# The scores' scaling and the experts' numbers of the slots with one operand in PSUM

## The chip, the cores and the metric

The kernel runs on one core of a Trainium2 chip. Its time is the device time of one launch in microseconds. A core has five engines with a queue of instructions each, worked off in order: TensorE (PE, matrix products and transposes), VectorE (DVE), ScalarE (ACT), GpSimd (POOL) and SyncE (SP, which here only issues DMA transfers). An instruction waits at the head of its queue until those whose results it needs have signalled.

## The reference

The input is `x` of 4 images, 384 channels, 32 x 32 positions, in fp32. Two layers follow, each a mixer and a feed-forward part with residual sums:

```python
x = x + selective_scan_block(ln_c(x))        # 4 scan directions, 16 states, softplus, norm, gelu
t = to_tokens(x)
scores = ln_t(t) @ gate_w + gate_b           # 4 experts
probs = softmax(scores)
masked = probs of the two best, normalised
t = t + sum_e masked[e] * (gelu(ln_t(t) @ w1[e] + b1[e]) @ w2[e] + b2[e])
x = x + attention(ln_c(from_tokens(t)))      # 8 heads of 64
t = to_tokens(x)
t = t + gelu(ln_t(t) @ kron(c_fc_1, c_fc_2).T) @ kron(c_proj_1, c_proj_2).T
```

The change lies in the routing: the scores, and the list that says which expert's weights each slot of tokens takes.

## The kernel before

**The stages.** The scan is done for the four images (batches) in turn. A batch has 4 directions in 2 halves of 512 positions, so there are 32 units; a unit has 3 chunks of 128 channels and 4 groups of states, so there are 384 groups in all. A group works so: ACT makes the decays `da` in PSUM (L443), POOL multiplies `bx` (L434, twice a group), DVE runs the recurrences (L448, four times, and small copies of the carries, L454 and L459), POOL and DVE multiply by the output coefficients (L462 once, L455 twice), and PE adds up the states (L469, eight matmuls in the profile). Between the units lie the projections (L332, L359, L389 to L398). The coefficients come back from DRAM, spread over the partitions, by DMA on SP (`bcs` L344, `dtr` L418).

**The tail of a batch** runs beside the scan of the next ones:
- `route`, called for batch 0 by itself and for batch b + 1 inside the tail of batch b: `spread` (from L620) transposes the tokens (L641), takes raw scores from the same bank (L643), statistics (L654, L655), and 1/sqrt of the variance by ACT as `rstd` (L151, L152). Then it scales the scores (L658), adds the bias (L659), makes `less`, the negative product of mean and rstd (`less_mean`, L546 and L547), and calls `places`. POOL then scatters the normalised tokens to rows sorted by expert with 16 indirect transfers (L675), each about 1.27 us after the one before.
- `places` (L682 to L847) does some sixty small DVE operations on tiles of at most 128 columns: ranks of the experts, counts, the position of each token (`pos`, L818), its weight (L846), and at the end the expert of each slot (`expert`, L844). Its scratch `area` is one PSUM bank of tag `o`, which `small` cuts up; what isn't in `area` is in SBUF.
- `experts`: 11 slots a batch, each with a fetch of 8 weight blocks of 576 KB on SP, whose address is loaded from `expert` (L858), a gather of token rows (`xs`, L891), transposes (L900), two products (L921 and L937), and a store.
- `combine` gathers the two rows of each token on POOL (L967), weighs and adds them on PE (L975) and DVE (L979). `prologue` normalises (stats, `less_mean`, L992) and transposes (L999). Then come `attention` (projection L1024, scores L1047, exponentials L1052, sums L1096) and `last_layers` (L1144, z L1163, hidden layer L1184, f_acc L1197, output L1207 and L1211).

**What sets the order.** The program is written once and a scheduler with a model of the engines' times then places each instruction in its engine's queue. So the order of all queues depends on what the model makes of every operation, and instructions far from an edit move with it. Routing, combining and the last layers have high priority. Tiles are shared by tags: `p`, `o` and `s` are PSUM banks, and with one buffer of tag `p` while the scan runs, `less_ps`, `cnt_ps`, `fo_ps` and others take turns; `o` holds `places`, `y_ps`, `o_acc` or `f_acc`.

In the text a "group" is one of the 384 scan groups, numbered by the L469 matmuls of PE's queue. Line numbers are those of the kernel before.

Of the kernel before, what the change touches and what calls it, by code (L numbers as in the profile page):

```python
# [12 lines left out]
ALU = mybir.AluOpType  # L13
AX = mybir.AxisListType
# [3 lines left out]
P = 128  # L18
# [14 lines left out]
NE = 4  # L33
# [8 lines left out]
NFULL = TOP * L // SLOT  # L42
NHALF = (NROW - NFULL * SLOT) // P
# [6 lines left out]
MB = L // P  # L50
# [65 lines left out]
class Body:  # L116
# [425 lines left out]
    def less_mean(self, mean, rstd, room, tag):  # L542

        less = room.tile([P, MB], tag, "less")
        ps = room.bank("p", "less_ps")[:, :MB]
        self.nc.scalar.copy(ps, rstd)  # L546
        self.nc.vector.scalar_tensor_tensor(less, mean, -1.0, ps, op0=ALU.mult, op1=ALU.mult)  # L547
        return less

# [68 lines left out]
    def spread(self, b, x1, room):  # L620


        nc = self.nc
        src = x1[b].rearrange("(c p) l -> p c l", p=P)
        st = room.tile([P, MB, 6], "r_st", "st")
        mv = room.tile([P, MB, 2], "r_mv", "mv")
        rstd = room.tile([P, MB], "r_rstd", "rstd")
        sc = room.tile([P, MB, NE], "sc", "sc")


        for m in [*range(MB // 2, MB, 2), *range(0, MB // 2, 2)]:
            x = room.tile([P, DC, 2 * P], "k4", "x")
            nc.sync.dma_start(out=x, in_=src[:, :, m * P : (m + 2) * P])
            xt = room.tile([P, 2, D], "k4", "xt")

            both = room.two("tt_ps") if b == 0 else None
            for o in range(2):
                ps = room.bank("p", "tt_ps") if both is None else both[:, o, :]
                cols = slice(o * P, (o + 1) * P)
                for c in range(DC):  # L640
                    nc.tensor.transpose(ps[:, c * P : (c + 1) * P], x[:, c, cols], self.ident)  # L641
                for c in range(DC):
                    nc.tensor.matmul(  # L643
                        ps[:, D : D + NE], x[:, c, cols], self.wg[:, c, :],
                        start=(c == 0), stop=(c == DC - 1),
                    )
                if both is None:
                    nc.scalar.copy(xt[:, o, :], ps[:, :D])
                    nc.vector.tensor_copy(sc[:, m + o, :], ps[:, D : D + NE])
            if both is not None:  # L650
                nc.scalar.copy(xt, both[:, :, :D])
                nc.vector.tensor_copy(sc[:, m : m + 2, :], both[:, :, D : D + NE])
            for o in range(2):
                nc.vector.bn_stats(st[:, m + o, :], xt[:, o, :])  # L654
                nc.vector.bn_aggr(mv[:, m + o, :], st[:, m + o, :])  # L655
            nc.sync.dma_start(out=self.tokens(b)[:, m : m + 2, :], in_=xt)
        self.inverse_root(rstd, mv[:, :, 1], self.eps5)
        nc.vector.tensor_mul(sc, sc, rstd.unsqueeze(2).to_broadcast([P, MB, NE]))  # L658
        nc.vector.tensor_add(sc, sc, self.bg.unsqueeze(1).to_broadcast([P, MB, NE]))  # L659
        less = self.less_mean(mv[:, :, 0], rstd, room, "r_less")  # L660
        pos, gate, expert = self.places(sc, room)

        placed = []
        for m in range(MB):
            if m % 2 == 0:
                xt = room.tile([P, 2, D], "k4", "xt")
                nc.sync.dma_start(out=xt, in_=self.tokens(b)[:, m : m + 2, :])
            nc.scalar.activation(  # L670
                xt[:, m % 2, :], xt[:, m % 2, :], AF.Identity,
                bias=less[:, m : m + 1], scale=rstd[:, m : m + 1],
            )
            for k in range(TOP):
                put = nc.gpsimd.indirect_dma_start(  # L675
                    out=self.rows[b][:, :],
                    out_offset=bass.IndirectOffsetOnAxis(ap=pos[:, k, m : m + 1], axis=0),
                    in_=xt[:, m % 2, :], in_offset=None,
                ).ins
                for other in placed:  # L680
                    self.tc.declare_no_dep(put, other, reason="rows of different tokens")
                for other in self.zeroed:  # L682
                    self.depend(put, other)
                placed.append(put)
        return (pos, gate), (expert, placed)

    def places(self, sc, room):


        nc = self.nc  # L690
# [51 lines left out]
        ps = room.bank("p", "cnt_ps")  # L742
# [27 lines left out]
        first = room.tile([P, 2, NE + 1], "g_first", "g_first")  # L770
        nc.vector.memset(first[:, :, :1], 0.0)
        for e in range(NE):
            nc.vector.tensor_add(first[:, :, e + 1], first[:, :, e], used[:, :, e])
        pairs, odd = first[:, 0], first[:, 1]
        more = room.tile([P, 1], "g_more", "g_more")
# [14 lines left out]
            op0=ALU.mult, op1=ALU.add,  # L790
# [13 lines left out]
            op0=ALU.mult, op1=ALU.add,  # L804
# [14 lines left out]

        def later(n, before, name):
            flags = room.tile([P, n, NE - 1], "g_" + name, "g_" + name)
            nc.vector.tensor_tensor(
                flags, self.slot_at[:, :n].unsqueeze(2).to_broadcast([P, n, NE - 1]),
                before[:, 1:NE].unsqueeze(1).to_broadcast([P, n, NE - 1]), op=ALU.is_ge,
            )
            return flags

        ef = room.tile([P, NSLOT], "g_ef", "g_ef")  # L830
        nc.vector.tensor_reduce(
            ef[:, : NFULL + 1], later(NFULL + 1, pairs, "later"), AX.X, ALU.add
        )
        half = room.tile([P, 2, NHALF], "g_half", "g_half")
        nc.vector.tensor_reduce(half[:, 0], later(NHALF, odd, "lone"), AX.X, ALU.add)
        nc.vector.tensor_sub(
            half[:, 1, :2], ef[:, NFULL : NFULL + 1].to_broadcast([P, 2]), half[:, 0, :2]
        )
        nc.vector.tensor_sub(half[:, 1, 2:], half[:, 0, : NHALF - 2], half[:, 0, 2:])
        nc.vector.scalar_tensor_tensor(  # L840
            ef[:, NFULL:], half[:, 1], more, half[:, 0], op0=ALU.mult, op1=ALU.add
        )
        expert = room.sb.tile([P, NSLOT], I32, tag="g_expert", name="g_expert", bufs=2)
        nc.vector.tensor_copy(expert, ef)  # L844
# [140 lines left out]
    def prologue(self, xt, xn, room):  # L985


        nc = self.nc
        mean, rstd = self.stats(xt, self.eps6, room)
        less = self.less_mean(mean, rstd, room, "less")  # L990
        for m in range(MB):
            nc.scalar.activation(  # L992
                xn[m], xt[:, m, :], AF.Identity, bias=less[:, m : m + 1], scale=rstd[:, m : m + 1]
            )
        xc = room.tile([P, DC, L], "k12", "xc")
        for c in range(DC):
            ps = room.two("tc_ps")
            for m in range(MB):
                nc.tensor.transpose(  # L999
                    ps[:, m // 4, m % 4 * P : (m % 4 + 1) * P], xn[m][:, c * P : (c + 1) * P],  # L1000
                    self.ident,
                )
            nc.scalar.copy(xc[:, c, :], ps.rearrange("p o l -> p (o l)"))
        return xc
# [443 lines left out]
```

## Time and profile before

| | |
|---|---|
| three runs | 4393.62, 4397.94, 4407.22 us; median 4397.94 |
| the profiled execution | 4396.59 us; span in the profile 4394.8 us |
| granted TensorE clock, mean | 0.852 |
| busy | PE 78%, POOL 69%, DVE 66%, ACT 56%, weight loads 37% |
| last scan step of DVE (L455) ends | 3517 us |
| first expert transposes (L900) of batches 0, 1 and 3 | 910, 1940 and 3615 us |
| traffic | 684.81 MB by DMA, mean 156 GB/s |

How to read it: the page gives busy time by engine, the span in 40 slices with the busy share in tenths, the chain of work that ended last, and the costliest groups of instructions with their mean length and the idle time before them. A row of a timeline has the start in us, the length, engine, line, operation, output and inputs, shape and count, and in brackets how long the engine stood idle before it and what ended that. In group rows the last columns are busy us, mean ns of one, and idle us before. An instruction's length runs from its start to its end as the profiler records them, so a wait for something other than a semaphore is part of the length.

### The profile page before, as it was taken

The numbers are of one execution on the slowest core, as the hardware profiler recorded it, in microseconds if no ns is written. First come the engines' busy times: TensorE is split into PE (matmuls) and PEld (weight loads), VectorE is DVE, ScalarE is ACT, GpSimd is POOL, SyncE is SP. The second block draws the span as 40 slices with busy tenths as digits, with TensorE's granted clock in tenths as the row PEclk, the third lists the DMA queues.
The fourth block names the chain that finished last, engine by engine and source line by source line (L and its number), as shares of the span: only waits on it lengthen the run. The fifth ranks groups of instructions, "written<-read, shape, count | busy, mean of one in ns | idle before, by whom it ended". The sixth has DMA issues, their size and how long they took to land.

```text
span 4394.8 us, 47123 instructions
## 1 busy us (share of the span) xinstructions
PE 3448.4 (78%) x13980; PEld 1647.6 (37%) x13980; DVE 2901.9 (66%) x4256; ACT 2479.0 (56%) x4402; POOL 3050.7 (69%) x1475
## 2 busy tenths in 40 slices
PE   6545545479996897679997888758998789999997
PEld 2111113145553232235554322314555435556433
DVE  5889996878866868968887677978787720002102
ACT  4545554456655766566675567466666543343554
POOL 4999996889878969788998788878898810000100
PEclk7676665589997989689998889768999899999998
DMA  4444463487776534557788534446789543344200
GB/s 121 122 124 114 115 176 87 132 245 218 228 215 200 153 94 130 143 182 212 221 237 254 155 96 121 118 152 179 220 232 260 187 153 105 115 133 158 94 17 15
DMA packets 404760, 684.81 MB, mean 156 GB/s; under 512 B 50960, under 2 KB 206480, under 8 KB 404496
## 3 DMA queue, kind: packets, MB, share of 16 engines
q1 hardware_dynamic: 395184, 655.37, 51.9%
q0 software_dynamic: 8192, 25.17, 1.8%
q8 instruction: 112, 1.84, 0.2%
q14 instruction: 152, 1.25, 0.1%
q10 hardware_dynamic: 1120, 1.18, 0.1%
HBM read 561.47 MB, written 120.06 MB: 155 GB/s over the span
## 4 chain that ended last, share of the span: by engine, by line
PE 39%; DVE 23%; ACT 11%; POOL 9%; DMA 9%; issue 7%; SPq 2%; DVEq 0%; POOLq 0%; ACTq 0%
PE y_ps L937 8%; PE h_ps L921 8%; DVE da L448 8%; DVE bx L448 8%; POOL bx L434 4%; PE s_ps L1047 4%; DMA dtr<-dd 4%; PE o_acc L1096 4%; ACT da L443 3%; PE acc L469 3%; DVE bx L455 3%; POOL bx L462 2%; PE xd_ps L332 2%; DMA w<-in_w 2%; PE w_ps L1024 1%
## 5 line engine op out<-in xcount | busy, mean ns | idle before, releaser
L434 POOL TENSOR_TENSOR bx<-dtr,bcs 128x1024 f32<-128x1024 f32 x768 | 1793.7, 2360 | 237.4 <-PE acc L469 138.3
L443 ACT ACTIVATE da<-dtr,nega 128x512 f32<-128x512 f32 x1536 | 1045.0, 690 | 991.2 <-DVE bx L455 577.6
L462 POOL TENSOR_TENSOR bx<-bx,bcs 128x1024 f32<-128x1024 f32 x384 | 904.6, 2360 | 162.6 <-DVE carry L459 67.7
L469 PE MATMUL acc<-bx,sel 128*32 128x512 f32 x3072 | 509.9, 706 | 285.7 <-POOL bx L462 246.8
L921 PE MATMUL h_ps<-xc,w 128*128 128x256 f32 (+1 forms) x3168 | 661.6, 363 | 45.3 <-DMA w<-in_w 22.1
L937 PE MATMUL y_ps<-w,hs 128*128 128x384 f32 x1824 | 644.8, 507 | 66.4 <-ACT hs L930 58.7
L921 PEld LDWEIGHTS h_ps<-xc,w 128*128 128x128 f32 x3168 | 544.3, 196 | 226.6 <-issue 83.4
L448 DVE TENSOR_TENSOR_SCAN bx<-da,carry,bx 128x512 f32<-128x512 f32 x384 | 473.6, 1270 | 110.1 <-POOL bx L434 59.1
L448 DVE TENSOR_TENSOR_SCAN bx<-da,bx 128x512 f32<-128x512 f32 x384 | 453.0, 1211 | 118.0 <-POOL bx L434 58.6
L448 DVE TENSOR_TENSOR_SCAN da<-da,carry,bx 128x512 f32<-128x512 f32 x384 | 477.6, 1274 | 78.6 <-ACT da L443 61.0
L455 DVE TENSOR_TENSOR bx<-da,bcs 128x512 f32<-128x512 f32 x768 | 510.1, 680 | 4.3
L448 DVE TENSOR_TENSOR_SCAN da<-da,bx 128x512 f32<-128x512 f32 x384 | 455.3, 1218 | 65.3 <-ACT da L443 43.9
L937 PEld LDWEIGHTS y_ps<-w,hs 128*128 128x128 f32 x1824 | 350.1, 197 | 358.9 <-issue 74.3
L1052 ACT ACTIVATE ex<-s_ps 128x512 f32<-128x512 f32 x512 | 299.5, 591 | 254.2 <-PE s_ps L1047 253.0
L1047 PE MATMUL s_ps<-w 64*128 64x512 f32 x1024 | 306.5, 675 | 74.5 <-ACT ex L1052 74.1
L1137 POOL TENSOR_TENSOR xt<-xt,wb 128x3072 f32<-128x3072 f32 x4 | 26.8, 6692 | 406.6 <-DMA wb<-in_wb 406.6
L469 PEld LDWEIGHTS acc<-bx,sel 128*32 128x32 f32 x3072 | 78.9, 116 | 590.0 <-POOL bx L462 345.9
L1096 PE MATMUL o_acc<-ex,vt 128*64 128x512 f32 x1024 | 293.4, 651 | 0.0
L926 ACT ACTIVATE hs<-h_ps,bb 128x256 f32<-128x256 f32 (+1 forms) x528 | 193.7, 445 | 106.9 <-PE h_ps L921 105.3
L1047 PEld LDWEIGHTS s_ps<-w 64*128 64x128 f32 x1024 | 80.5, 192 | 243.7 <-ACT ex L1052 143.0
L941 DVE TENSOR_TENSOR y<-y_ps,bb 128x384 f32<-128x384 f32 x76 | 41.8, 550 | 196.5 <-PE y_ps L937 195.2
L359 PE MATMUL dt_ps<-xd,wdt 12*128 12x512 f32 x192 | 123.7, 729 | 53.6 <-ACT mag L398 27.4
(220 smaller groups left out, 3868.0 us busy)
## 6 DMA issues: line engine op xcount, KB each, us to landing
w<-in_w SPq DMA_DIRECT2D x352, 576.0 KB
dtr<-dd SPq DMA_DIRECT2D x1536, 128.0 KB
bcs<-rows SPq DMA_DIRECT2D x512, 128.0 KB
dd<-one_e SPq DMA_DIRECT2D x96, 256.0 KB
dd<-mag SPq DMA_DIRECT2D x96, 256.0 KB
rows<-zero SPq DMA_DIRECT2D x76, 192.0 KB
xs<-rows SPq DMA_DIRECT2D x32, 384.0 KB
made<-y SPq DMA_DIRECT2D x32, 384.0 KB
```

The lines of the kernel that those rows point to most:

```text
L434: pool = nc.gpsimd.tensor_mul(bx, dtr[q][1], bc[:, 0].unsqueeze(1).to_broadcast([P, 2, HF])).ins
L443: nc.scalar.activation(da, dtr[q][0][:, j, :], AF.Exp, scale=nega[:, col : col + 1])
L448: nc.vector.tensor_tensor_scan(run(h), run(da), run(bx[:, j, :]), 0.0 if first else hold, ALU.mult, ALU.add,)
L455: dve = nc.vector.tensor_mul(bx[:, j, :], h, cg).ins
L462: pool = nc.gpsimd.tensor_mul(bx, bx, cg.unsqueeze(1).to_broadcast([P, 2, HF])).ins
L469: nc.tensor.matmul(acc[lo : lo + DB, :], sel, out[q][:, j, :], start=(g == 0), stop=(g == NG - 1),)
L921: nc.tensor.matmul(ps[:, r, :], w1[(f + r) // wf][:, c, (f + r) % wf * P : ((f + r) % wf + 1) * P], xc[:, c, :], start=(c == 0), stop=(c = ...
L926: nc.scalar.activation(hs[:, f + r, :], ps[:, r, :], AF.Identity, bias=bb[:, f + r : f + r + 1])
L937: nc.tensor.matmul(out[:, :D], hs[:, f, t * P : (t + 1) * P], w2[f // wf][:, f % wf, :], start=(f == 0), stop=(f == FC - 1),)
L1047: nc.tensor.matmul(ps[:, o, :], w[rows, j * P : (j + 1) * P], w[rows, halves(i)], start=True, stop=True,)
L1052: ins = nc.scalar.activation(ex[:, o, :], ps[:, o, :], AF.Exp, scale=HD**-0.5, accum_out=sums[:, t, 2 * j + o, i : i + 1],).ins
L1096: ins = nc.tensor.matmul(out[cols, :], made[t][1][:, j, cols], ex[:, o, :], start=(j == 0), stop=(j == MB - 1),).ins
```

## The change

Three edits, all on DVE's operands:
- `less_mean` now also returns its PSUM bank, which holds ACT's copy of `rstd`. `spread` calls it ahead of the scaling, multiplies the scores by that copy, writes the product into the same bank, and adds the bias from there into `sc`. The product `less` is computed first, the scaling after it.
- In `places` the two lists of first slots, `first`, are copied into `area` (`starts`), and the comparisons with the slot numbers (L824) read that copy.
- The reduction of `lone` is done twice, into `half[:, 0]` in SBUF as before and into `last` in `area`; the three operations behind it (L836, L839, L840) take `last` as one operand.

```diff
     def less_mean(self, mean, rstd, room, tag):
 
         less = room.tile([P, MB], tag, "less")
-        ps = room.bank("p", "less_ps")[:, :MB]
-        self.nc.scalar.copy(ps, rstd)
-        self.nc.vector.scalar_tensor_tensor(less, mean, -1.0, ps, op0=ALU.mult, op1=ALU.mult)
-        return less
+        ps = room.bank("p", "less_ps")
+        self.nc.scalar.copy(ps[:, :MB], rstd)
+        self.nc.vector.scalar_tensor_tensor(
+            less, mean, -1.0, ps[:, :MB], op0=ALU.mult, op1=ALU.mult
+        )
+        return less, ps
...
         self.inverse_root(rstd, mv[:, :, 1], self.eps5)
-        nc.vector.tensor_mul(sc, sc, rstd.unsqueeze(2).to_broadcast([P, MB, NE]))
-        nc.vector.tensor_add(sc, sc, self.bg.unsqueeze(1).to_broadcast([P, MB, NE]))
-        less = self.less_mean(mv[:, :, 0], rstd, room, "r_less")
+        less, ps = self.less_mean(mv[:, :, 0], rstd, room, "r_less")
+        scaled = ps[:, MB : MB + MB * NE].rearrange("p (m e) -> p m e", e=NE)
+        nc.vector.tensor_mul(scaled, sc, ps[:, :MB].unsqueeze(2).to_broadcast([P, MB, NE]))
+        nc.vector.tensor_add(sc, scaled, self.bg.unsqueeze(1).to_broadcast([P, MB, NE]))
         pos, gate, expert = self.places(sc, room)
...
+        starts = small([P, 2, NE + 1])
+        nc.vector.tensor_copy(starts, first)
+
...
         nc.vector.tensor_reduce(
-            ef[:, : NFULL + 1], later(NFULL + 1, pairs, "later"), AX.X, ALU.add
+            ef[:, : NFULL + 1], later(NFULL + 1, starts[:, 0], "later"), AX.X, ALU.add
         )
         half = room.tile([P, 2, NHALF], "g_half", "g_half")
-        nc.vector.tensor_reduce(half[:, 0], later(NHALF, odd, "lone"), AX.X, ALU.add)
+        lone, last = later(NHALF, starts[:, 1], "lone"), small([P, NHALF])
+        nc.vector.tensor_reduce(half[:, 0], lone, AX.X, ALU.add)
+        nc.vector.tensor_reduce(last, lone, AX.X, ALU.add)
         nc.vector.tensor_sub(
-            half[:, 1, :2], ef[:, NFULL : NFULL + 1].to_broadcast([P, 2]), half[:, 0, :2]
-        )
-        nc.vector.tensor_sub(half[:, 1, 2:], half[:, 0, : NHALF - 2], half[:, 0, 2:])
+            half[:, 1, :2], ef[:, NFULL : NFULL + 1].to_broadcast([P, 2]), last[:, :2]
+        )
+        nc.vector.tensor_sub(half[:, 1, 2:], half[:, 0, : NHALF - 2], last[:, 2:])
         nc.vector.scalar_tensor_tensor(
-            ef[:, NFULL:], half[:, 1], more, half[:, 0], op0=ALU.mult, op1=ALU.add
+            ef[:, NFULL:], half[:, 1], more, last, op0=ALU.mult, op1=ALU.add
         )
```

More of the change, by code (lines that the diff above doesn't have):

```diff
@@ L989, in prologue @@
         mean, rstd = self.stats(xt, self.eps6, room)
-        less = self.less_mean(mean, rstd, room, "less")
+        less, _ = self.less_mean(mean, rstd, room, "less")
         for m in range(MB):
```

## The prediction

> **What bounds the kernel now.** First the page: busy shares, the slices, the chain that ended last, the costliest groups.
>
> ```profile
> PE 3448.4 (78%) x13980; PEld 1647.6 (37%) x13980; DVE 2901.9 (66%) x4256; ACT 2479.0 (56%) x4402; POOL 3050.7 (69%) x1475
> ...
> PE   6545545479996897679997888758998789999997
> ...
> DVE  5889996878866868968887677978787720002102
> ...
> POOL 4999996889878969788998788878898810000100
> ...
> PE 39%; DVE 23%; ACT 11%; POOL 9%; DMA 9%; issue 7%; SPq 2%; DVEq 0%; POOLq 0%; ACTq 0%
> ...
> L434 POOL TENSOR_TENSOR bx<-dtr,bcs 128x1024 f32<-128x1024 f32 x768 | 1793.7, 2360 | 237.4 <-PE acc L469 138.3
> ...
> L462 POOL TENSOR_TENSOR bx<-bx,bcs 128x1024 f32<-128x1024 f32 x384 | 904.6, 2360 | 162.6 <-DVE carry L459 67.7
> ```
>
> There are two regimes. Until slice 32 (3517 us) the scan runs with DVE and POOL at seven to nine tenths; after that PE alone is full. The scan is 384 equal groups (two L434 and one L462 on POOL, 7.1 us, in each); in the units without other work a group takes 6.9 to 7.4 us, so POOL sets it there. Elsewhere it takes 8.5 to 10.9 us, because routing, experts and attention of the batch before share the engines. No single engine bounds that part, and the chain hops between all of them.
>
> Second, the routing of batch 0, 836 to 883 us: DVE's groups by shape in that window, then POOL's timeline.
>
> ```profile
> L658 DVE TENSOR_TENSOR sc<-sc,rstd 128x32 f32<-128x32 f32 x1 | 3.5, 3482 | 0.0
> L839 DVE TENSOR_TENSOR g_half<-g_half 128x1 f32<-128x1 f32 x1 | 2.4, 2370 | 0.0
> L824 DVE TENSOR_TENSOR g_lone<-slot_at_i,g_first 128x9 f32<-128x9 f32 x1 | 2.4, 2356 | 0.0
> L836 DVE TENSOR_TENSOR g_half<-g_ef,g_half 128x2 f32<-128x2 f32 x1 | 2.3, 2298 | 0.0
> L840 DVE SCALAR_TENSOR_TENSOR g_ef<-g_half,g_more 128x3 f32<-128x3 f32 x1 | 2.3, 2261 | 0.0
> L824 DVE TENSOR_TENSOR g_later<-slot_at_i,g_first 128x27 f32<-128x27 f32 x1 | 1.9, 1917 | 0.0
> ...
> L788 DVE TENSOR_SCALAR g_full<-g_more 128x4 f32<-128x4 f32 x1 | 1.0, 979 | 0.0
> ...
> L715 DVE TENSOR_TENSOR places<-sc,places 128x32 f32<-128x32 f32 x1 | 0.2, 196 | 0.0
> ...
> L659 DVE TENSOR_TENSOR sc<-sc,bg 128x32 f32<-128x32 f32 x1 | 0.2, 191 | 0.0
> ```
>
> ```profile
> 848.66 2.36 POOL L462 TENSOR_TENSOR bx<-bx,bcs 128x1024 f32<-128x1024 f32 x1 [8.44 <-DVE carry L459]
> ...
> 871.85 4.63 POOL L434 TENSOR_TENSOR bx<-dtr,bcs 128x1024 f32<-128x1024 f32 x2
> 882.93 1.18 POOL L675 DMA_INDIRECT rows<-xt,g_pos  x1 [6.45 <-DVE g_weight L846]
> ```
>
> A subtraction on one column (L839) takes 2.37 us, just the length of one POOL product (2.36), while L715, a 128x32 product with one operand in PSUM, takes 0.196. All six slow rows have both inputs in SBUF and ran while POOL was busy; L659, in the stretch where POOL idled 8.44 us, has two SBUF inputs too and took 0.191. So these rows are waits for POOL, not work. POOL then idles 6.45 us for the positions.
>
> Third, PE's timeline where the experts of batch 0 start, and where the scan ends.
>
> ```profile
> 910.23 1.54 PE L900 MATMUL xc_ps<-ident,xs 128*128 128x128 f32 x6 [19.85 <-DMA xs<-rows]
> ...
> 914.26 12.35 PE L921 MATMUL h_ps<-xc,w 128*128 128x256 f32 x56
> ```
>
> ```profile
> 3501.21 4.67 PE L999 MATMUL tc_ps<-ident,got 128*128 128x128 f32 x8 [5.98 <-ACT got L992]
> ...
> 3522.94 1.13 PE L1047 MATMUL s_ps<-w 64*128 64x512 f32 x4
> ...
> 3615.45 1.54 PE L900 MATMUL xc_ps<-ident,xs 128*128 128x128 f32 x6 [9.70 <-DMA xs<-rows]
> ```
>
> PE stands 19.85 us for the gathered rows with scan matmuls (L469) behind it in its queue, and 9.70 us again for batch 3.
>
> **Part by part.** *The waits.* The slow rows per batch, from DVE's timeline. Batch 0: 3.48 + 1.92 + 2.36 + 2.30 + 2.37 + 2.26 = 14.69 us. Batch 1: L658 1.61 and L824 0.93. Batch 2: L659 0.88, L836 2.31, L840 0.45. Batch 3: none, POOL is idle. In their place stand operations with one PSUM operand; the nearest rows are L715 (0.196) and L785 (0.15), so 0.15 to 0.2 each. Added: the copy of `first` into PSUM (nearest, the copies of a column out of PSUM, L454: 0.15) and a second reduction of `g_lone` (L835: 0.15), 0.31 a batch. DVE saves 14.69 - 1.02 - 0.31 = 13.4 us in batch 0, 2.54 - 0.37 - 0.31 = 1.9 in batch 1, 3.64 - 0.50 - 0.31 = 2.8 in batch 2 and loses 0.3 in batch 3. Around the last two routings DVE is at 0.97 and more, so I count them whole.
>
> The new copy has one SBUF input. L788, one SBUF input and an SBUF output, took 0.98 and 1.15 us in batches 0 and 2 against 0.16 elsewhere, so such an operation can wait too; upper bound 3 x 2.36 us, below nothing is excluded because it is added work. I take 0.15, since an operand in PSUM is what it has in common with the fast rows. The Trainium skill (VectorE: DVE Perf Modes, Why PSUM operands drop a tier) says that an operand in PSUM shuts out the two-port modes, which would make this copy free of the wait; read with SBUF — State Buffer, Who interferes with whom, where a copy can take the shared ports, it would be 3 x 1 us dearer. No row of before has a copy from SBUF to PSUM.
>
> A rule that speaks against the change: elementwise work on a PSUM source should rather be copied to SBUF first when many operations follow (VectorE: DVE Perf Modes, Rules for kernel authors). Here L715 with PSUM (196 ns) and L659 without (191 ns) differ by 5 ns, so by the row the seven new PSUM reads cost 0.04 us.
>
> *The scaling now waits for ACT's copy of rstd and for a bank of tag p.* L546 took 0.17 us; in batch 3 DVE's L547 followed rstd by 0.6 us, so 0.6 us a batch, on DVE in front of queued scan steps; the bank is held until the addition, one product later. 0 to 2 us a batch; 0.6 is inside the stages below.
>
> *What moves.* In the built order the positions (L818) now come before the experts' numbers (L844), and in batches 0 to 2 two to eight scan steps of DVE stand between them. The weights' fetches on SP wait for L844, the scatter on POOL (L675) for L818. For batch 0: the positions are ready 14.9 us sooner, but POOL still has its products ahead of the scatter. Its 8.44 us of idling shrinks by L658's 3.3, and from 848.66 to 876.48 it works without a pause, so the scatter starts at about 873.2 instead of 882.93: 9.7 us, not 14.9. The gather of `xs` on SP now stands behind eight loads of `bcs`, which came when POOL's first two products after the scatter ended (906.7 and 909.0); less 9.7, plus 2.1 to issue four, that is 901.4, and L900 follows 4.5 us later (905.77 to 910.23): 905.9, 4.3 us sooner, with two scan groups more already done, since PE's order now has L900 behind group 107 instead of 105. The rest of the saving is in those two groups.
>
> *The slip of the tail against the scan.* Everything behind is replanned. Counting scan groups in front of the same instruction on PE: first expert transposes 105, 213, 326 before, 107, 220, 329 after; first attention projection 160, 271, 381 before, 164, 276, 384 after. So scan groups per stage change by +2 (before the experts of batch 0, priced above), +2 (experts 0), +3 (attention and last layers 0), -2 (experts 1), -2 (attention 1), 0 (experts 2), -3 (the tail); in all nought. A group costs at least PE's part, 1.8 us (1.06 for eight L469, and shares of L359 and L332), and at most the mean length of a group there, 9.1 us in expert stages and 10.4 in attention stages. In the expert stages PE is at 0.9 to 0.98 and POOL at 0.8 to 0.96, so I take 4.5, between PE's part and POOL's 7.1; in the attention stages 7.1. That gives +9, +21, -9, -14: 7 us lost (bounds: 2 and 10).
>
> *The end.* Before, from the first combining matmul of batch 2 (3472) to the first scores (3522.9) are 51 us with four scan groups between; now two stand behind the first combining matmuls and none behind the projection. Combining took 20 us, the normalisation and transposes 25 without the interleaved scan matmuls: 45, 6 us less. Batch 3's routing starts at the scan's end, and attention of batch 2 now starts later against it, so the 9.70 us wait at L900 goes; late next is PE's own work. 15.7 us (bounds 4 and 16).
>
> Sum: -4.3 + 7 - 1.9 - 2.8 - 15.7 = -17.7 us. Bounds: -4.3 + 2 - 4.7 - 16 = -23, and -4.3 + 10 - 4.7 - 4 = -3. The profiled execution took 4396.6 (span 4394.8), 1.3 under the median of 4397.9: 4396.6 - 17.7 = 4379, 4380 on the median's footing.
>
> **The rivals.** *The slip is paid and not given back* (slower). If the five groups that the experts and the attention of batch 0 take on cost the full 9.1 and 10.4 us (+18, +31) and the later stages, which run by their own chains of DMA and ACT, don't get shorter, the sum is -4.3 + 49 - 4.7 - 15.7 = +24: 4421. For it: in the attention stages PE, ACT and DVE are all short of full, so length comes from chains of waits; L1197 waits 13.75 us for the routing's bank at 1860, and the experts' numbers now release that bank some 8 us after the positions. Against it: POOL's 7.1 us a group leave room. It decides from a cost of 22 us for what the later stages don't give back.
>
> *The waits were cover* (no change). POOL, not DVE, may set the pace while routing: then only the gap of 6.45 us counts, given up again by the slip: -6.5 + 7 = 0, 4397. Against it: POOL idles 14.9 us in that window, both times for DVE.
>
> *The slip costs nothing* (faster still). If the two groups at L900 were only blocked by PE's wait of 19.85 us and an added group costs PE's part alone: -23 from the bounds, and the wait of 5.9 us at L900 in batch 1 goes as well: -29, 4368.
>
> *It doesn't do what it says*: L840 keeps `g_half` and `g_more` in SBUF; if a column operand counts as a second SBUF input, 2.1 + 0.3 us stay. L448 with `carry` as column takes 1.27 against 1.21 without, over 384 each while POOL ran: it doesn't wait. Inside the range.
>
> **How the numbers follow.** Forecast -17.7 with its bounds: 0.38; slip free 0.14; no change 0.20; slip paid 0.28. About 0.3% (13 us) is what a measurement of this kernel can tell from no change. Faster by more: most of the first (0.36 of 0.38) and the second: 0.50. Within: 0.22, from the third and the first's end at -3. Slower: 0.28. The range runs from 4354, under the second case by the 14 us by which executions of before spread, to 4416, which leaves out the dearest part of the fourth.
>
> **What would show it.** Right: L658's successor, both L824, L836, L839 and L840 at 0.2 us in all batches; the scatter of batch 0 near 873; its first L900 near 906 with a wait far under 19.85; no wait at batch 3's L900. Wrong: any of these still at 2.3 us; a stage from attention of batch 0 to the experts of batch 1 (545 us before, from 1381 to 1926) longer by over 30 us; the scan's last L455 later than 3517.

## The result, and the profile after

The changed kernel takes 4446.66 us (median of four: 4429.51, 4446.49, 4446.83, 4446.88) against 4396.2 us (four runs of the kernel before on the same chip): ratio 1.010, 95% interval 1.0071 to 1.0130. It is 1% slower, where 4380 us was predicted. The profiled execution is the 4429.51 one (span 4427.7, mean granted clock 0.854 against 0.852 before, so a lower clock is not what its 33 us come from); the others have spans of 4445 at 0.848 to 0.851, and their further 17 us are in neither of the two traces compared here. On a second chip the ratio was 1.0075 (1.0058 to 1.0093).

The page after: busy time, the slices of PE, DVE and POOL, the chain by engine, and the costliest POOL group.

```profile
PE 3454.1 (78%) x13980; PEld 1654.3 (37%) x13980; DVE 2888.8 (65%) x4264; ACT 2480.5 (56%) x4402; POOL 3049.6 (69%) x1475
...
PE   6545555479987887669998688667999789999997
...
DVE  5889997868886866968877577787887620002102
...
POOL 4999996888988968788988688879898710000100
...
PE 23%; DVE 7%; ACT 6%; DMA 3%; POOL 2%; issue 2%; SPq 1%; DVEq 0%; ACTq 0%; POOLq 0%
...
L434 POOL TENSOR_TENSOR bx<-dtr,bcs 128x1024 f32<-128x1024 f32 x768 | 1794.2, 2361 | 281.1 <-PE acc L469 179.5
```

DVE works 13.1 us less, as meant. No other engine has clearly more to do (PE 5.7 us in 3454, ACT 1.5). The loss is idle time: PE idles 27 us more (span less busy time: 973.6 instead of 946.4), and POOL stands 281.1 us before its scan products instead of 237.4, and 179.5 of it is for PE's L469 instead of 138.3. The chain was followed over 44% of the span only, so its shares don't compare with before.

DVE's groups in the routing of batch 0 (830 to 885 us). Lines are those of the changed kernel: L662 was L658, L830 was L824, and L844, L847, L848 were L836, L839, L840.

```profile
L791 DVE TENSOR_SCALAR g_full<-g_more 128x4 f32<-128x4 f32 x1 | 1.6, 1554 | 0.0
...
L848 DVE SCALAR_TENSOR_TENSOR g_ef<-g_half,g_more,places 128x3 f32<-128x3 f32 x1 | 0.2, 218 | 0.0
L662 DVE TENSOR_TENSOR less_ps<-sc,less_ps 128x32 f32<-128x32 f32 x1 | 0.2, 195 | 0.0
...
L826 DVE COPY places<-g_first 128x10 f32<-128x10 f32 x1 | 0.2, 172 | 0.0
L830 DVE TENSOR_TENSOR g_lone<-slot_at_i,places 128x9 f32<-128x9 f32 x1 | 0.2, 159 | 0.0
...
L830 DVE TENSOR_TENSOR g_later<-slot_at_i,places 128x27 f32<-128x27 f32 x1 | 0.2, 157 | 0.0
L844 DVE TENSOR_TENSOR g_half<-g_ef,places 128x2 f32<-128x2 f32 x1 | 0.2, 157 | 0.0
...
L847 DVE TENSOR_TENSOR g_half<-g_half,places 128x1 f32<-128x1 f32 x1 | 0.1, 149 | 0.0
```

All six waits are gone: 14.69 us have become 1.04. So the mechanism aimed at works, and what it bought was lost elsewhere. The start of the experts of batch 0, on POOL, SP's queue and PE (L678 was L675, L899 was L891, L908 was L900):

```profile
871.90 1.18 POOL L678 DMA_INDIRECT rows<-xt,g_pos  x1 [0.18 <-DVE g_expert L852]
```

```profile
901.08 3.60 SPq L344 DMA_DIRECT2D bcs<-rows  x8
905.00 0.38 SPq L899 DMA_DIRECT2D xs<-rows  x1
905.48 7.68 SPq L418 DMA_DIRECT2D dtr<-dd  x12
913.35 1.56 SPq L899 DMA_DIRECT2D xs<-rows  x1
```

```profile
895.68 1.93 PE L469 MATMUL acc<-bx,sel 128*32 128x512 f32 x8 [18.81 <-POOL bx L462]
...
910.74 1.54 PE L908 MATMUL xc_ps<-ident,xs 128*128 128x128 f32 x6 [10.82 <-DMA xs<-rows]
```

The scatter begins 11 us sooner, but the first gather leaves SP at 905.00 (before: 905.77) and the second at 913.35 (before: 908.45), because SP now has eight loads of `bcs` ahead of the first and twelve of `dtr` ahead of the second. PE starts the experts at 910.74, no sooner than before.

Stage by stage along the tail, in us of the two first traces (before, after). The stages are cut at the first expert transposes (L900) and the first attention projection (L1024) of each batch:

| stage | scan groups in it | length before | length after | change |
|---|---|---|---|---|
| to the first expert transposes of batch 0 | +2 | 910.2 | 910.7 | +0.5 |
| experts 0 | +2 | 508.8 | 524.4 | +15.6 |
| attention and last layers 0 | +3 | 520.7 | 561.1 | +40.4 |
| experts 1 | -2 | 509.1 | 532.2 | +23.1 |
| attention and last layers 1 | -2 | 558.7 | 522.4 | -36.3 |
| experts 2 | 0 | 501.8 | 502.5 | +0.7 |
| attention of batch 2 to the end | -3 | 885.5 | 874.4 | -11.1 |

The sum is +32.9, the difference of the spans. The scan itself ends at 3518.2 us instead of 3517.3: it has gained nothing from the tail's falling behind. What was still to do then took 909.5 us instead of 877.5. PE's timeline at the scan's end (L983 was L975, L1055 was L1047):

```profile
3517.83 5.51 PE L983 MATMUL w_ps<-got,diag 128*128 128x384 f32 x8 [10.18 <-DMA got<-made,g_pos]
...
3567.00 1.40 PE L1055 MATMUL s_ps<-w 64*128 64x512 f32 x4
```

Combining batch 2 up to the first scores takes 49 us. Before it took 51 (3472 to 3522.9) and lay under the scan's last groups; now it begins where the scan ends.

So work of PE has moved from under the scan to behind it. These are the sums of the engines' busy time from 3518 to 4430 us, that is behind the scan's end, before and after:

```profile
sum 912.00, PE 806.81 PEld 412.95 DVE 109.17 ACT 389.17 POOL 51.54; mean PE 73.35 PEld 37.54 DVE 9.92 ACT 35.38 POOL 4.69
```

```profile
sum 912.00, PE 833.28 PEld 424.50 DVE 119.56 ACT 396.84 POOL 68.70; mean PE 75.75 PEld 38.59 DVE 10.87 ACT 36.08 POOL 6.25
```

PE is busy for 26.5 us more there. Up to the scan's last step, which comes at the same time in both, it has done 73 matmuls fewer (2621.0 us busy instead of 2641.0).

### The profile page after: what moved, and what is told of

Read it like the earlier page. It is cut to its first block, busy times and chain, and to the rows that moved or that the text cites. A ratio compares the mean times of both kernels' runs of the same rounds, so it can differ in the third digit from the quotient of the medians.

```text
span 4427.7 us, 47146 instructions
## 1 busy us (share of the span) xinstructions
PE 3454.1 (78%) x13980; PEld 1654.3 (37%) x13980; DVE 2888.8 (65%) x4264; ACT 2480.5 (56%) x4402; POOL 3049.6 (69%) x1475
## 5 line engine op out<-in xcount | busy, mean ns | idle before, releaser
L434 POOL TENSOR_TENSOR bx<-dtr,bcs 128x1024 f32<-128x1024 f32 x768 | 1794.2, 2361 | 281.1 <-PE acc L469 179.5
L462 POOL TENSOR_TENSOR bx<-bx,bcs 128x1024 f32<-128x1024 f32 x384 | 902.9, 2357 | 160.1 <-DVE carry L459 72.6
L469 PE MATMUL acc<-bx,sel 128*32 128x512 f32 x3072 | 494.7, 700 | 319.9 <-POOL bx L462 267.7
L1055 PE MATMUL s_ps<-w 64*128 64x512 f32 x1024 | 308.7, 679 | 91.3 <-ACT ex L1060 91.1
L469 PEld LDWEIGHTS acc<-bx,sel 128*32 128x32 f32 x3072 | 77.5, 116 | 614.7 <-POOL bx L462 370.0
L1055 PEld LDWEIGHTS s_ps<-w 64*128 64x128 f32 x1024 | 81.5, 194 | 269.6 <-ACT ex L1060 163.9
```

The costliest lines, as they stand in the source:

```text
L434: pool = nc.gpsimd.tensor_mul(bx, dtr[q][1], bc[:, 0].unsqueeze(1).to_broadcast([P, 2, HF])).ins
L462: pool = nc.gpsimd.tensor_mul(bx, bx, cg.unsqueeze(1).to_broadcast([P, 2, HF])).ins
L469: nc.tensor.matmul(acc[lo : lo + DB, :], sel, out[q][:, j, :], start=(g == 0), stop=(g == NG - 1),)
L1055: nc.tensor.matmul(ps[:, o, :], w[rows, j * P : (j + 1) * P], w[rows, halves(i)], start=True, stop=True,)
```

## The experiments

**What could be the cause.** The planner (the scheduler that places the instructions) keeps the operations on one bank in the order of the program. In the kernel before, the experts' numbers (L824 to L844) never touch `area`, and in batch 0 DVE runs the first of them at 864.2 us, ahead of the positions (L818, 882.5). With `starts` and `last` in `area` they come behind (869.2 after 867.8). So the edit has two parts: operands, and an order that the planner builds anew for all queues. Theory A: the order costs. B: the operands or their banks cost. C: any edit moves the plan by a per cent, at random. Ratios are against the kernel before, measured beside it on the same chip; its median lay between 4404 and 4439 us on the five chips of the experiments. Times in the expectations of the first four runs are on the footing of 4397 us, so they are compared by their ratios.

**c_early**: the changed kernel with the block of the experts' numbers written ahead of the positions.

```diff
+        starts = small([P, 2, NE + 1])      # ... up to the cast into `expert`
         at = cnt[:, 0]
         ...
-        starts = small([P, 2, NE + 1])      # ... up to the cast into `expert`
         weight = room.tile([P, TOP, nt], "g_weight", "g_weight")
```

> The changed kernel whole, all its PSUM operands kept, but the experts' numbers (from the copy of `first` into the bank up to `expert`) are written ahead of the positions, so that in DVE's queue they come before L818's positions again as they did before; with that the built order has the first expert transposes behind scan groups 105, 213 and 326 and the attention behind 160, 271 and 381, the very numbers of the kernel before (107, 220, 329 and 164, 276, 384 in the changed kernel). Theory A, the loss comes from the order (the bank's accesses stay in program order, so the experts' numbers are tied behind the positions and the whole tail is planned later): the 33 to 50 us are gone and what is left is the gain of the waits, 4375 to 4397. Theory B, the loss comes from the PSUM operands or the banks that they hold: it stays at 4430 to 4450. Theory C, the planner's order is a matter of chance and any edit moves it by a per cent: same order as before, so near 4397 too; C is told from A by the other runs.

Measured: 4434.34 against 4437.39 us, 0.9995 (0.9984 to 1.0006). The loss is gone, as A has it, and B falls: every PSUM operand is still there. A gain of the waits isn't to be seen either.

**b_places**: the places' half of the change alone; `spread` and `less_mean` as before.

```diff
+        starts = small([P, 2, NE + 1])
+        nc.vector.tensor_copy(starts, first)
...
+        nc.vector.tensor_reduce(last, lone, AX.X, ALU.add)
```

> The part in the slots' experts alone (copy of `first` into the bank, second reduction, operands in PSUM); the scaling is the one of the kernel before, on SBUF. Built order: 107, 220, 329 groups before the experts, 164, 276, 384 before the attention, as in the changed kernel. A: the loss comes whole with this part, 4430 to 4455 (the scaling's 3.5 and 1.6 us waits are back, which is 5 us at most). B, if it is the scaling's bank of tag p, held until the addition, that costs: 4385 to 4405. C: 4430 to 4455, since the order is the changed kernel's.

Measured: 4476.01 us, 1.0084 (1.0066 to 1.0102). The loss comes with this half.

**j_late**: the kernel before, with the two comparisons (L824) tied behind the positions by order alone.

```diff
+        placed = nc.vector.tensor_copy(pos, picked[:, 0]).ins
 ...
+            self.tc.add_manual_dep(op.ins, placed.name, <no semaphore>, reason="order")
             return flags
```

> The kernel before, every operand where it was, but the flags of the slots' experts (L824) are given an order behind the positions (L818) on DVE's queue, with no semaphore between: the place that the changed kernel has for them. Built order: 107, 219, 328 before the experts, 163, 274, 381 before the attention, 195 and 307 before the last layers. A: most of the loss without any PSUM operand, 4420 to 4450. B: no loss, 4390 to 4405. C: anything from 4370 to 4440.

Measured: 4452.43 us, 1.0030 (1.0019 to 1.0041). Slower without any new operand, but by a third of the changed kernel's loss, and below what A expected (0.5 to 1.2%). The planner made another plan of it (last layers of batch 0 behind 195 groups, 199 in the changed kernel).

**a_scale**: the scaling's half alone; `places` as before.

```diff
+        nc.vector.tensor_mul(scaled, sc, ps[:, :MB].unsqueeze(2).to_broadcast([P, MB, NE]))
+        nc.vector.tensor_add(sc, scaled, self.bg.unsqueeze(1).to_broadcast([P, MB, NE]))
```

> The scaling alone (rstd's copy in PSUM taken by L658's successor, product in PSUM, bank given back after the addition); the slots' experts as in the kernel before, ahead of the positions. Built order: 105, 212, 321 groups before the experts, 160, 265, 375 before the attention, 192 and 300 before the last layers, so the tail runs up to six groups earlier than before. A: the waits of 3.5, 1.6 and 0.9 us are gone and the tail comes earlier rather than later: 4380 to 4400. B, the bank costs: 4410 to 4450. C: 4370 to 4440.

Measured: 4439.52 us, 0.9997 (0.9984 to 1.0010). The scaling and its bank cost nothing, and gain nothing that can be measured. Nor does the tail's earlier place in this plan (up to six groups) gain anything.

**Order and operands apart.** In these kernels all five queues are held to a sequence written down beforehand, by edges that carry no semaphore. The sequence is the place of each instruction in the plan of the kernel before or of the changed one.

```diff
         with tc.If(over > 0):
             body.second_layer_exact()
+        tie(nc, tc)     # one edge from each instruction to the one before it in its engine's list
```

**x_base**, the control for all of them:

> The kernel before with its queues held, by the same kind of order edges, to the sequence that they have anyway. All theories: within 0.15% of the kernel before; if not, the edges themselves cost, and every kernel held by them must be read against this one.

Measured: 4438.5 against 4439.44 us, 1.0004 (0.9988 to 1.0020). The edges cost nothing beyond this interval.

**base** and **after2**, the two kernels as they are, on the chip of the next two:

> The kernel before itself, unchanged, on the same chip as the three others, for a trace that theirs can be set against. All theories: equal to its own repeats within 0.3%.

> The changed kernel unchanged, on the same chip as the two others: the yardstick. All theories: 0.7 to 1.3% over the kernel before, as at first.

Measured: base 4406.43 us beside 4404.04, its trace spans 4404.7 us. after2 4440.68 us, 1.0075 (1.0058 to 1.0093), its trace spans 4443.1 us.

**x_order**: old operands, new order.

> The arithmetic and operands of the kernel before (scaling and slots' experts on SBUF, no second reduction, no copy into the bank), but all five engines' queues are held, by order edges without semaphores, to the very sequence that the changed kernel's queues have (its two added instructions left out, every other instruction in its place). A (the order costs): the whole loss and a few us more, since the waits of the kernel before stay: 1.0 to 1.5% over the kernel before. B (the operands cost): no loss, within 0.3%. If 0.3 to 0.7%: both have a share.

Measured: 4445.67 us, 1.0090 (1.0074 to 1.0106).

**x_ops**: new operands, old order.

> The counterpart: all PSUM operands, the copy and the second reduction of the changed kernel, but all five queues are held to the very sequence of the kernel before (the copy of `first` just ahead of the first flags, the second reduction just behind the first one; the addition after less in batch 3). A: nothing of the loss; the routing's positions of batch 0 come some 10 to 14 us sooner, and either that reaches the end, 0.2 to 0.4% faster, or it is swallowed by the next wait, within 0.2%. B: 0.7 to 1.3% slower. Which group of the scan the gain ends at, if it is swallowed, is read from its trace against that of the kernel before.

Measured: 4396.43 us, 0.9978 (0.9968 to 0.9988). Together:

| | old order | new order |
|---|---|---|
| old operands | 1 | 1.0090 |
| new operands | 0.9978 | 1.0075 |

This settles A against B: the same order loses with either kind of operands. The order loses 0.9 to 1.0%. The operands gain 0.22% in the old order; in the new one the gain of 0.15% lies within the intervals. What C says of the planner isn't settled by it: the tie's price differs from plan to plan. But each kernel with the tie in its plan lost (b_places, j_late and, below, k_starts), and the two that keep the experts' numbers ahead of the positions (c_early, a_scale) did not. x_ops beats both kernels. Its positions of batch 0 come 10.5 us sooner than in base (882.15 to 871.63); the gain at scan group 108 is 10 us, it shrinks to 3 at group 222, and it is 13 us at the scan's end, where 9.8 us of it reach the end of the trace. base and x_order, with the same operands, repeat the pattern of the stages: experts 0 +20.5 us, attention and last layers 0 +48.3, experts 1 +18.3, attention and last layers 1 -36.8, experts 2 +3.1; and behind the scan's last step PE is busy for 832.2 us instead of 808.3.

**Where in the order.** Old operands throughout. A cut takes one kernel's order up to a scan group, and the other's for all that is left:

```diff
-QUEUE = the order of one kernel
+QUEUE = that order up to the group, then what is left, in the order of the other
```

Theory E: the loss is the uncovered chain at the end. Theory S: it is made in the stages between.

**s_late**, old order up to group 290, new behind it, and **s_early**, the reverse:

> Operands of the kernel before. All queues in its own order up to the scan's 290th group, behind that in the order of the changed kernel: the slip of batches 0 and 1 is left out, that of batch 2 is in (experts of batch 2 behind 329 groups instead of 326, combining behind 382 instead of 380, its attention behind 384 instead of 381). Theory E (end): the loss is that the combining chain of batch 2 no longer lies under the last scan groups, so from the scan's last step to the end it takes 905 to 913 us instead of 878, and the whole is 0.5 to 0.9% slower. Theory S (stages): the loss is made in attention of batch 0 and at the change to the experts of batch 1, where the order of the kernel before stands here: within 0.2%.

> The counterpart: all queues in the order of the changed kernel up to the scan's 290th group, behind that in the order of the kernel before, so the tail's late work is put in ahead of the scan at once and batch 2 stands as before (326, 380, 381). E: from the scan's last step to the end 876 to 882 us again; what is left is the later end of the scan, 0 to 0.4% slower. S: 0.7 to 1.1% slower.

Measured: s_late 4450.57 against 4433.44 us, 1.0033 (1.0020 to 1.0046); s_early 4484.06 us, 1.0111 (1.0092 to 1.0131). From the scan's end to the end of the trace s_late takes 929.9 us and s_early 888.2, on the same chip. So the end does get 42 us longer by the late slip, and part of that comes back as an earlier scan end: 13 us in this trace (3530 against an estimated 3543), whose execution lies 11 us above the median, and some 25 by the medians, which are 17 us apart; and in s_early, where the end is mended, the scan ends at 3594 us, some 50 us late (an estimate: the kernel before, at 4433 us and with the same 888 us behind its scan, would end it near 3543). E alone falls.

**s_end**, old order up to group 366:

> Operands of the kernel before. Its own order up to the scan's 366th group, behind that the order of the changed kernel: only the last 18 groups are dealt out otherwise, the combining of batch 2 behind 382 groups instead of 380 and its attention behind 384 instead of 381. E: from the scan's last step to the end 900 to 913 us instead of 878; the scan may end up to 20 us sooner, since its last groups stand ahead of experts' work: 0.2 to 0.9% slower. S: within 0.2%. A third, that late tail work and early scan work only change places: the scan's end sooner by as much as the rest is longer, within 0.1%.

Measured: 4444.21 us, 1.0022 (1.0009 to 1.0035). The rest behind the scan is 929.1 us, the scan ends at 3518 us: against the same estimate 41 us longer and 25 us sooner, so largely an exchange, of which 11 us are not given back by the medians.

**k_starts**: the kernel before with the copy of `first` into `area` as its only edit, which ties the numbers behind the positions and moves the tail further.

```diff
+        starts = small([P, 2, NE + 1])
+        nc.vector.tensor_copy(starts, first)
-            ... later(NFULL + 1, pairs, "later") ... later(NHALF, odd, "lone")
+            ... later(NFULL + 1, starts[:, 0], "later") ... later(NHALF, starts[:, 1], "lone")
```

> The kernel before with nothing but the copy of `first` into the bank and the flags reading it there; no other PSUM operand. It ties the experts' numbers behind the positions as well, and the planner makes more of it: experts of batch 2 behind 336 groups, combining and attention behind all 384, last layers of batch 1 behind 313. E, by dose: the tail is some 7 groups later at the scan's end than in the changed kernel, from the scan's last step to the end 930 to 1000 us, 1.2 to 2.5% slower. S: the same early slip as the changed kernel (107, 164, 199, 220, 276), so the same loss, 0.7 to 1.1%. Chance alone: anything from 0 to 2%.

Measured: 4528.51 us, 1.0219 (1.0194 to 1.0245), with 974.2 us behind the scan's end. With the experts of batch 2 behind 336 groups instead of 329 the loss is more than twice that of the changed kernel, though the early slip is the same. E's dose is met; S alone falls too.

**Cuts further forward.** Two places were suspected: the start of the experts of batch 0 (T1; T2 says that it costs nothing lasting), and the last layers of batch 0 with the routing of batch 1. **l135 and l205** (old order up to that group, new behind it), **e135** (new order up to it, old behind):

> Operands of the kernel before; all queues in its own order up to the scan's 135th group (start of the experts of batch 0 as before, the first transposes behind group 105), behind that in the changed kernel's order (attention of batch 0 behind 164, experts of batch 1 behind 220). T1 (the start of the experts of batch 0 holds some 29 of the loss): 0.3 to 0.65% over the kernel before, against 0.9% for the whole new order. T2 (the start costs nothing that lasts; the loss comes later): 0.75 to 1.05%.

> As the last, but the kernel before's order up to the 205th group, so that routing, experts, attention and the routing of batch 1 up to its positions lie as before and the new order begins with the experts of batch 1 (behind 220). If the last layers of batch 0 and the routing of batch 1 hold the second part (some 30 us): 0.2 to 0.45%, about what the cut at group 290 gave (0.33%). If they hold none: the same as the cut at 135.

> The counterpart of l135: the changed kernel's order up to the 135th group (first expert transposes behind group 107), the kernel before's behind that. T1: 0.25 to 0.6% slower. T2: within 0.15%.

Measured against 4407.15 us: l135 4448.28, 1.0088 (1.0072 to 1.0105); l205 4443.45, 1.0079 (1.0063 to 1.0095); e135 4418.66, 1.0023 (1.0012 to 1.0034). The first place doesn't hold: leaving out the bad start of the experts of batch 0 saves nothing that can be measured (T2). Alone it costs 0.23%, between the two expectations. The second place holds no loss either: l205 has the old order there and loses as much as l135.

**x_sp**: x_order with the two gathers put back in SP's queue, which reads, around them:

```diff
-  bcs bcs bcs bcs bcs bcs bcs bcs xs0 dtr (x12) xs1
+  xs0 bcs bcs bcs bcs xs1 bcs bcs bcs bcs dtr (x12)
```

> Operands of the kernel before in the changed kernel's order (0.9% slower), with one thing put back: in SP's queue the first gather of rows (xs) of batch 0 stands ahead of the eight loads of bcs again instead of behind them, and the second one between them instead of behind twelve loads of dtr. T1 by this mechanism: first expert transposes 6 to 12 us sooner than in x_order, second slot some 10 us sooner, and 0.45 to 0.75% slower than the kernel before. If PE was held by POOL's products, not by the gathers: no change, 0.8 to 1.0%.

Measured: 4442.97 us, 1.0078 (1.0063 to 1.0093). In the traces the first expert transposes come 4.8 us sooner than in x_order and the end 9.4, but the two ran on different chips; by the ratios it is 0.12%, with overlapping intervals. The gathers' place costs time where it stands; that it reaches the end isn't settled.

**l240**: old order up to group 240, which lies in the middle of the experts of batch 1.

> Operands of the kernel before, its own order up to the 240th group (experts of batch 1 begin behind 213 as before), the changed kernel's order behind that (attention of batch 1 behind 276 instead of 271, experts of batch 2 behind 329 instead of 326). If the half per cent hangs on the start of the experts of batch 1: 0.25 to 0.45%, as with the cut at 290. If any slip in the middle costs it, because the scan groups that then run without tail work still take POOL's 7 us each: 0.6 to 0.85%, as with the cut at 205.

Measured: 4469.31 against 4439.44 us, 1.0069 (1.0050 to 1.0087), as expected if any slip in the middle costs it. x_base ran on the same chip, so the two traces show the slip by itself: same queues up to group 240, and behind it l240 has scan groups where x_base has experts' work. All engines from 2180 to 2235 us, x_base first (columns: stretch and its length, busy time of each engine with its instructions, granted clock, DMA share, GB/s):

```profile
core 0: us, PE busy (x) PEld busy (x) DVE busy (x) ACT busy (x) POOL busy (x), PEclk, DMA share, GB/s
2180.00:2235.00 55.00, 53.28 (x229) 32.40 (x228) 45.95 (x75) 37.61 (x63) 52.00 (x25) 1.00 0.76 212
```

```profile
2180.00:2235.00 55.00, 30.95 (x115) 13.54 (x113) 49.58 (x80) 29.90 (x48) 51.49 (x25) 0.75 0.47 122
```

Two rows of that stretch by line, first x_base, then l240, and PE's waits of l240 for POOL there (us in total, times, longest):

```profile
L921 PE MATMUL h_ps<-xc,w 128*128 128x256 f32 x112 | 25.7, 384 | 0.7 <-DVE carry L459 0.7
...
L462 POOL TENSOR_TENSOR bx<-bx,bcs 128x1024 f32<-128x1024 f32 x7 | 16.6, 2367 | 0.4 <-DVE carry L459 0.4
```

```profile
L462 POOL TENSOR_TENSOR bx<-bx,bcs 128x1024 f32<-128x1024 f32 x7 | 16.4, 2346 | 2.5 <-DMA rows<-xd 2.5
...
L921 PE MATMUL h_ps<-xc,w 128*128 128x256 f32 x52 | 13.5, 424 | 0.0
```

```profile
PE acc L469 <- POOL bx L462: 14.2, 4, 8.5
```

Both do seven groups in 55 us (seven L462, one a group): 7.9 us each, at POOL's pace, with POOL busy for 52 us. In x_base PE does 112 L921 beside them (and 48 L937), in l240 52 (and none). With 52 of 160 of the experts' matmuls left a group takes no less; PE idles for 24 us instead of 2, 14.2 of it for POOL's products, and runs at a clock of 0.75 instead of 1.00. It is so over a longer way too: the 24 groups from 240 to 264 take 201 us in l240 and 199 in x_base, with 456 and 576 matmuls of the experts (L921, L937) beside them. Later l240 gets only 7.4 us of it back (scan end 3531.5 instead of 3538.9), while the rest behind the scan is 37.4 us longer (928.5 instead of 891.1): +30, the 0.69%.

So the cause: the new order lets scan groups go ahead of the tail in PE's queue. In the stretch of l240 the scan is paced by POOL and the tail's PE work rides under it. What is moved out from under it is done later, in the changed kernel behind the scan's end (26.5 us more of PE there), where PE is busy for 833 of 912 us and the scan no longer runs beside it. Catching up later in a lump (s_early, 1.1%) costs no less.

Open: why the planner makes so much of one tie (0.3% in j_late, 2.2% in k_starts), and why the same slip costs 0.33% from group 290 and about 0.7% from 240 on. Open too is how the loss falls on the single stages: the experts of batch 1 took 23.1 us longer with two groups fewer. And the length behind the scan alone is no measure of it: c_early, without loss, has 909.7 us there behind a scan end of 3524.9, a_scale on the same chip 887.5 behind 3550.1. A cut also makes a jump of its own, so the cuts' shares can't be added up.

## Why the prediction was wrong, by its own steps

*The waits.* Right. Six rows were to fall from 14.69 to 1.02 us and fell to 1.04; copy and second reduction were to cost 0.31 and cost 0.33. One size is off: L791 (L788 before), one SBUF operand, waited for 1.55 us instead of 0.98. The new copy was the row for which the prediction had two readings of the Trainium skill. By VectorE: DVE Perf Modes (Why PSUM operands drop a tier) an operand in PSUM keeps an operation out of the mode that needs both read ports, so no wait. SBUF — State Buffer (Who interferes with whom) lets a copy contend with GpSimd only when its operands meet the conditions of that mode; the prediction left them out and put 3 us on this reading, from L788's row. The copy took 0.157 to 0.172 us in all four batches, so the first reading held.

*Positions and scatter.* Right: positions 14.7 us sooner (14.9 said), scatter at 871.9 (873.2 said).

*First expert transposes, -4.3.* Measured +0.5, 4.8 us off. The loads of `bcs` began at 901.08 instead of 899.3 (1.8 us); eight of them were to be issued ahead of the gather, where the issue of four was counted (3.9 us instead of 2.1); and from the gather to the transposes it took 5.7 us instead of 4.5. The second gather behind twelve loads of `dtr` was not looked at.

*The slip, +7 with bounds of 2 and 10.* **This is the step that failed.** The five stages of it measure 15.6 + 40.4 + 23.1 - 36.3 + 0.7 = +43.5, which is 36.5 of the 50.6 us between the forecast (-17.7) and the measured difference of the spans (+32.9). A group was priced at 4.5 us beside experts, between PE's own part (1.8) and POOL's (7.1), and the same price was credited where stages lose groups, so that a slip summing to nought cost next to nothing. Batch 0 paid 56.0 us for five groups, 11.2 each, over the upper price of 9.1 to 10.4. Batch 1 gave back 13.2 us for four, 3.3 each, and that in a sum of opposite signs: the experts of batch 1 were to get 9 us shorter and got 23.1 longer. The bounds of 2 and 10 came from the same symmetry, so they could not hold this. l240 shows why it isn't symmetric: a group without tail work takes POOL's time all the same, so nothing is won by moving it ahead, and PE's free time under it is lost.

*The end, -15.7, and the later waits, -4.7.* Measured -11.1 from the first projection of batch 2 on. The 9.70 us wait of batch 3 fell to 3.0 as said. Of the 6 us credited for the combining 1.7 came (51 to 49 us).

*The scan's end* as a sign of error (later than 3517) was no good sign: it came at 3518.2, and 32.0 of the 32.9 us are behind it. The other sign, attention of batch 0 to the experts of batch 1 longer by over 30 us, was right: by the marks of the table 520.7 us became 561.1.

*The rivals.* "The slip is paid and not given back" is what happened: its slip of +49 is near the 43.5 measured. Stage by stage it is near by luck: attention 1 did get 36.3 us shorter and the experts of batch 1 longer, and its reason, chains of DMA and ACT in the later stages, is not what l240 shows. Its total of 4421 is short of the 4429.5 of the profiled execution since it kept the -4.3 and the -15.7; the median lies higher still. It had 0.28. "It doesn't do what it says" falls: L848 keeps `g_half` and `g_more` in SBUF and took 0.218.

## What to carry to other kernels

Putting an operand into a tile that others write ties it into the order of that tile, and a planner may redo every queue for it; price the edit's operands and its order apart, by holding the queues to the old order, before judging it. Where one engine paces a stage, work of the other engines that rides under it is free only there: a slip that nets to nought in groups still costs what is pushed out from under the pace and has to be done where nothing runs beside it. So price a moved group by what each side can do without the other, not by one price both ways.

## What the hardware showed

The granted clock moved with PE's load inside one stage: 1.00 in the stretch with PE busy for 53 of 55 us, 0.75 in the one with 31, and an L921 took 424 ns there instead of 384. Between chips the same kernel differed by 0.8% (4404.04 to 4439.44 us), with mean granted clocks of 0.852 and 0.848.
